# Two halves of an image mixer on one Trainium2 core: second images of one half beside the first images of the other, first modes of both at once, earlier parameters, larger loads

## Chip, cores, metric

The kernel runs on 1 core of one Trainium2 chip. The metric is device time in microseconds (us), lower is better. All runs compared here are of the fast state. In the text PE is TensorE (matmul), DVE is VectorE, ACT is ScalarE, SP is SyncE, whose queue issues most loads; a "half" is 128 of the 256 channels, or, of a tile, 1024 of its 2048 columns; "modes" are the low frequencies of the images. Of the tiles, gs holds the modes of one block, yA the forward products of one block, Yd is the copy of these in device memory, YT that copy loaded again, and f1ps the products made from YT; g10 and g11 are the syntheses of the first modes of half 0 and half 1, g20 and g21 those of the second modes.

## The reference, cut to what matters

```python
# layer 0 (attention over rows) makes x1; neither it nor the first part of layer 1 changes
attn = instance_norm(attn + tokens, attn_norm_w, attn_norm_b)      # the kernel's y, scaled by lam
attn = attn.reshape(b * (C // 4), 4, H, W)                          # four channels are mixed
h0 = instance_norm(attn, norm2_w, norm2_b)
h1 = fno_layer(h0, mix_wr[0], mix_wi[0], ..., (H, W), norm=True, act=True)   # first modes, first images
h2 = fno_layer(h1, mix_wr[1], mix_wi[1], ..., (H, W), norm=True)             # second modes, second images
out = instance_norm(h2, mon_w, mon_b) + attn
return x1 + out
# fno_layer: forward FFT, 32x16 modes times weights, inverse FFT, norm, plus a 1x1 skip; act is gelu
```

Each group of four channels is on its own, so the kernel works on two halves of the channels in turn.

## The kernel before

```python
def first_modes(a):                     # spectrum of half a, synthesis to Gd1 in device memory
    ...                                 # scalars, scaling of Fy, products (mix_modes)
    synth_modes(wp, psum, Zj, P, h.Gd1, f"g1{a}")          # 16 stores on the SP queue

def first_images(a):
    def begin(b):
        ...                             # y block: resident for a == 0 and b >= 4, else a 1 MB load
        load_modes(gs, h.Gd1, b)
        ps = [psk.tile([P, 512], FP, tag="k", ...) for j in range(4)]
        skip(ps, by_turn(yt), h.bl0, False)
        image(ps, gs, bs4, slice(0, P))
        for j in range(4):
            nc.scalar.activation(by_turn(hb[b])[:, j], ps[j]..., AF.Gelu)
    for b in range(17):
        if b < 16:
            begin(b)
        if b > 0:
            ...                         # transposes, statistics, forward products of block b-1
            nc.scalar.copy(yA, psA)
            nc.scalar.dma_start(h.Yd[:, b - 1, :], yA)

def second_modes(a):
    for c in range(4):
        for hc in range(2):
            t = yp.tile([P, 2, 4, P], FP, tag="YT", ...)
            for j in range(4):
                for r in range(2):      # 64 loads of 64 KB a half, 32 partitions each
                    f0 = 32 * j + 16 * r + 4 * c
                    nc.sync.dma_start(t[32 * j : 32 * j + 32, r],
                        h.Yd[f0 : f0 + 4, 8 * hc : 8 * hc + 8, :].rearrange("f b (n t) -> (b n) f t", n=4))
        ...                             # f1ps: products with efwd, copied to F
    Z, left = mix_modes(wp, psum, F, 1, f"z{a}")
    synth_modes(gp, psum, [Z], P, h.Gd2, f"g2{a}")
    ...

def second_images(a):                   # pools: op bufs=2, opp bufs=8 (PSUM)
    for b in range(16):
        gs = wp.tile([P, 4, P], FP, tag="gs", ...);  load_modes(gs, h.Gd2, b)
        yt = wp.tile([P, NB], FP, tag="yt", ...);    nc.sync.dma_start(yt, ydv[:, a, px])
        xt = wp.tile([P, NB], FP, tag="xt", ...);    nc.sync.dma_start(xt, x1v[:, a, px])
        ps = [psk.tile([P, 512], FP, tag="k", ...) for j in range(4)]
        skip(ps, by_turn(hb[b]), blk[1], False)
        image(ps, gs, bs4, slice(0, P))
        for j in range(4):
            nc.scalar.activation(by_turn(hb[b])[:, j], ps[j]..., AF.Identity, bias=c0, scale=kap)
        nc.vector.scalar_tensor_tensor(xt, yt, lam, xt, ALU.mult, ALU.add)
        nc.vector.tensor_tensor(xt, xt, hb[b], ALU.add)
        nc.scalar.dma_start(outv[:, a, px], xt)

for a in range(2):
    first_modes(a); first_images(a); second_modes(a); second_images(a)
```

## Time and profile before

| | before |
|---|---|
| median, range of 3 runs | 3392.2 us, 3390.0 to 3397.3 |
| profiled run | span 3403.0 us |
| layer 0 and attention of layer 1, not touched | up to 2182 us |
| y of both halves, from its first to its last product | 264 us |
| first modes, first images, second modes, second images of half 0 | 72, 140, 89, 167 us |
| the same of half 1 | 58, 138, 85, 166 us |

A row of the windows view, as the prediction shows it, gives one stretch of the span. One reads it from the right: a high DMA share (0.89 in second images) suggests that transfers are the bound (the runs below show that it need not be so), a PE time close to the length (124.14 of 140.00 us in first images) suggests that PE is, and a row in which neither is high (40.77 of 71.70 us and 0.24 in first modes) suggests a chain of dependent steps. A row of the waits view names who waited, what ended the wait, and total, count and longest.

### The profile page before, as it was taken

Reading aid. Unit: us, or ns where it says so; the run is one execution under the profiler, and the core shown is the slowest. Engines: PE = TensorE matmul, PEld = TensorE weight load, DVE = VectorE, ACT = ScalarE, POOL = GpSimd, SP = SyncE. Lnnn points to the kernel's source line nnn. Section 1 sums busy time; section 2 is a strip of 40 time slices with the busy share of each in tenths; the row PEclk is TensorE's granted clock in tenths of the full one; section 3 lists DMA queues with packets and bytes.
Section 4 is the critical chain, followed back from the end, with each engine's and each line's share of the span. In section 5 each row is a group of like instructions: output and inputs, shape, how many; then the busy total and the mean of one; then the engine's idle time right before and its main releaser. Section 6 shows DMA issues by size and latency. Waiting matters only on the chain. (4 is left out here: it accounts for less than half of the span.)

```text
span 3403.0 us, 71671 instructions
## 1 busy us (share of the span) xinstructions
PE 2964.7 (87%) x30109; PEld 2003.0 (59%) x30109; DVE 1908.9 (56%) x2848; ACT 1240.2 (36%) x2277; POOL 1002.0 (29%) x807
## 2 busy tenths in 40 slices
PE   6799999999999999999996785989967776569675
PEld 5577777777777777777774474744443344344444
DVE  7566666666666666666665125746654434435344
ACT  0355555555555555555552001100013212133022
POOL 0255555555555555555552002000000000000000
PEclk9899999999999999999997955999978877589765
DMA  9222212111111111111110000278723248654298
GB/s 372 93 62 62 62 62 62 62 62 60 63 59 62 62 60 62 62 62 62 62 53 13 0 20 0 87 282 294 291 69 125 76 152 324 236 185 161 87 330 329
DMA packets 224524, 398.55 MB, mean 117 GB/s; under 512 B 23589, under 2 KB 181752, under 8 KB 197064
## 3 DMA queue, kind: packets, MB, share of 16 engines
q1 hardware_dynamic: 210376, 318.43, 28.0%
q10 hardware_dynamic: 13824, 75.50, 5.6%
q8 instruction: 239, 3.92, 0.5%
q14 instruction: 85, 0.70, 0.1%
HBM read 259.63 MB, written 134.22 MB: 116 GB/s over the span
## 5 line engine op out<-in xcount | busy, mean ns | idle before, releaser
L263 POOL TENSOR_TENSOR e<-e,b1T 128x1024 f32<-128x1024 f32 x256 | 609.4, 2381 | 104.5 <-ACT e L261 104.4
L282 DVE RECIPROCAL rd<-av 128x256 f32<-128x256 f32 x256 | 448.2, 1751 | 0.0
L284 POOL TENSOR_TENSOR og<-t,rd 128x256 f32<-128x256 f32 x256 | 185.8, 726 | 612.1 <-PE sc L253 593.9
L312 ACT COPY U<-u 128x129 f32<-128x129 f32 x256 | 99.4, 388 | 719.4 <-DVE stats L311 719.4
L281 DVE SCALAR_TENSOR_TENSOR t<-gate,av 128x256 f32<-128x256 f32 x256 | 107.9, 422 | 401.0 <-ACT gate L244 383.3
L262 DVE TENSOR_TENSOR e<-sc,b1T 128x1024 f32<-128x1024 f32 x256 | 309.0, 1207 | 2.5 <-PE sc L253 2.5
L253 PE MATMUL sc<-qkT 32*128 32x256 f32 x4096 | 293.3, 400 | 0.1
L264 ACT ACTIVATE e<-e 128x1024 f32<-128x1024 f32 x256 | 276.0, 1078 | 0.5 <-DVE e L262 0.4
L275 PE MATMUL av<-e,v 128*32 128x256 f32 x4096 | 274.7, 385 | 0.5 <-POOL e L263 0.5
L261 ACT ACTIVATE e<-sc 128x1024 f32<-128x1024 f32 x256 | 271.5, 1060 | 3.8 <-PE sc L253 3.7
L275 PE MATMUL av<-e,eb 128*32 128x256 f32 x4096 | 268.2, 379 | 0.0
L979 PE MATMUL yps<-xt,mpT 128*128 128x512 f32 x512 | 230.8, 604 | 11.6 <-issue 11.6
L287 POOL TENSOR_TENSOR xb<-xt,bo 128x256 f32<-128x256 f32 x256 | 187.0, 731 | 121.0 <-DMA kt<-in_L_conv_kv_x_dram 121.0
L240 DVE TENSOR_TENSOR v<-gv,eb 128x256 f32<-128x256 f32 x256 | 108.8, 425 | 198.6 <-PE gv L237 198.5
L944 PE MATMUL h2ps<-k_bsyn,gs 32*128 32x128 f32 x1024 | 128.7, 402 | 98.8 <-DMA gs<-Gd 98.7
L253 PEld LDWEIGHTS sc<-qkT 32*128 32x128 f32 x4096 | 184.9, 184 | 37.8 <-issue 0.6
L944 PEld LDWEIGHTS h2ps<-k_bsyn,gs 32*128 32x128 f32 x1024 | 119.9, 290 | 142.7 <-DMA gs<-Gd 116.5
L293 PEld LDWEIGHTS wo<-wo_half,og 128*128 128x128 f32 x1024 | 133.8, 190 | 107.0 <-issue 104.2
L275 PEld LDWEIGHTS av<-e,eb 128*32 128x32 f32 x4096 | 133.0, 110 | 88.2
L293 PE MATMUL wo<-wo_half,og 128*128 128x128 f32 x1024 | 182.7, 301 | 1.9 <-POOL og L284 1.9
L275 PEld LDWEIGHTS av<-e,v 128*32 128x32 f32 x4096 | 106.8, 109 | 129.8 <-ACT xnT L219 80.5
L1316 ACT ACTIVATE blocks<-h2ps,col 128x512 f32<-128x512 f32 x128 | 94.8, 776 | 236.0 <-PE h2ps L944 205.8
(494 smaller groups left out, 5393.8 us busy)
## 6 DMA issues: line engine op xcount, KB each, us to landing
y<-yd SPq DMA_DIRECT2D x52, 1024.0 KB
xb<-in_x_dram SPq DMA_DIRECT2D x32, 1024.0 KB
xt<-in_x_dram SPq DMA_DIRECT2D x128, 256.0 KB
kt<-in_L_conv_kv_x_dram SPq DMA_DIRECT2D x128, 256.0 KB
x1d<-x SPq DMA_DIRECT2D x256, 128.0 KB
xt<-x1d SPq DMA_DIRECT2D x32, 1024.0 KB
x<-x1d SPq DMA_DIRECT2D x32, 1024.0 KB
out_dram<-x ACTq DMA_DIRECT2D x32, 1024.0 KB
```

The source lines that it names most:

```text
L253: nc.tensor.matmul(sc[h // 2][:, h % 2, c * 256 : (c + 1) * 256], qkT[p, 256 + c * P : 256 + (c + 1) * P], qkT[p, 0:256], start=True, stop ...
L261: nc.scalar.activation(e[1], s1[1], AF.Exp)
L262: nc.vector.tensor_tensor(e[0], s1[0], b1[0], ALU.add)
L263: nc.gpsimd.tensor_tensor(e[1], e[1], b1[1], ALU.mult)
L264: nc.scalar.activation(e[0], e[0], AF.Exp)
L275: nc.tensor.matmul(ps[hd, den * 256 : (den + 1) * 256], w, r["e"][h // 2][:, h % 2, c, :], start=(c == 0), stop=(c == 1),)
L282: nc.vector.reciprocal(rd, ps[:, 256:512])
L284: nc.gpsimd.tensor_tensor(r["og"], t, rd, ALU.mult)
L287: nc.gpsimd.tensor_tensor(r["xb"], r["x"], bc(bo, 1, 2), ALU.add)
L293: nc.tensor.matmul(ps[:, j * P : (j + 1) * P], r["og"][:, j * P : (j + 1) * P], wo, start=True, stop=True)
L944: nc.tensor.matmul(ps[j][:, n * W : (n + 1) * W], gs[q, n, tt], bs[q, :], start=False, stop=(n == 3))
L979: nc.tensor.matmul(ps[j].rearrange("p (n w) -> p n w", w=W), mpT[:, sc, tt], by_turn(xt[:, sc])[:, j], start=(sc == 0), stop=False,)
```

## The change

The intent: first modes of both halves in one stage; the first half's output beside the second half's first images, since one is bound by transfers and the other by PE; parameters and the spectrum fetched in front of y; 16 loads of YT in place of 64; y and x1 in halves of a block, so that all of it fits.

```diff
+Fyd = dram.tile([P, 4, 2, NT], FP, name="Fyd")      # Fy stored here, loaded as F0 in front of y
...
-            def first_modes(a):
+            def first_modes():                        # both halves: one scaling, one mix_modes of width 256
...
+                        for a, h in enumerate(halves):
+                            synth_modes(wp, pss, Z[:, :, :, a * P : (a + 1) * P], P, h.Gd1, f"g1{a}", turned=True)
...
                     for b in range(17):
                         if b < 16:
+                            if beside is not None:
+                                beside(b, op, psk)
                             begin(b)
...
+                        YT = yp.tile([P, 2, 2, 16, P], FP, name=f"YT_{a}")
+                        for hc in range(2):
+                            for j in range(4):
+                                for r in range(2):
+                                    (nc.sync if r else nc.scalar).dma_start(
+                                        YT[32 * j : 32 * j + 32, hc, r],
+                                        h.Yd[32 * j + 16 * r : 32 * j + 16 * r + 16, 8 * hc : 8 * hc + 8, :].rearrange(
+                                            "f b (n t) -> (b n) f t", n=4))
...
-            def second_images(a):
+            def second_images(a, b, wp, psk):
+                for s in range(2):
+                    px = slice(b * NB + s * half, b * NB + (s + 1) * half)
+                    yt.append(wp.tile([P, half], FP, tag="yo", name=f"y4_{a}_{b}_{s}", bufs=2))
+                    nc.sync.dma_start(yt[s], ydv[:, a, px])
+                    xt.append(wp.tile([P, half], FP, tag="xo", name=f"x4_{a}_{b}_{s}", bufs=3))
+                    nc.sync.dma_start(xt[s], x1v[:, a, px])
+                gs = wp.tile([P, 4, P], FP, tag="gs3", name=f"gs3_{a}_{b}", bufs=2)
+                load_modes(gs, h.Gd2, b)
...
+            first_modes()
+            first_images(0)
+            second_modes(0)
+            first_images(1, beside=lambda b, wp, psk: second_images(0, b, wp, psk))
+            second_modes(1)
+            with tc.tile_pool(name="op", bufs=2) as wp, tc.tile_pool(name="opp", bufs=8, space=PSUM) as psk:
+                for b in range(16):
+                    second_images(1, b, wp, psk)
```

## The prediction

> **What bounds the kernel now.** I read the page's slices first. The change touches nothing before 2180 us, so I cut the rest, with the chain of work that ended last, into stages and asked for the busy time of each engine in each. The stages are: first half's y (the input of both halves' work), then for each half first modes, first images, second modes, second images. Columns: stretch; length; busy us of PE, weight loads, DVE, ACT, POOL; granted clock; DMA share; GB/s.
>
> ```profile
> 2215.00:2488.00 273.00, 263.96 (x1536) 126.98 (x1536) 156.05 (x252) 0.00 (x0) 0.00 (x0) 0.98 0.76 274
> 2488.00:2559.70 71.70, 40.77 (x588) 26.96 (x588) 34.56 (x101) 9.95 (x20) 0.00 (x0) 0.68 0.24 74
> 2559.70:2699.70 140.00, 124.14 (x1920) 58.01 (x1920) 72.44 (x113) 51.47 (x97) 0.00 (x0) 0.96 0.28 90
> 2699.70:2789.00 89.30, 54.21 (x676) 37.05 (x678) 25.91 (x56) 7.29 (x13) 0.00 (x0) 0.72 0.36 103
> 2789.00:2955.90 166.90, 102.07 (x948) 64.47 (x945) 74.30 (x32) 47.30 (x64) 0.00 (x0) 0.64 0.89 325
> 2955.90:3013.60 57.70, 37.43 (x582) 23.95 (x582) 23.59 (x45) 8.08 (x15) 0.00 (x0) 0.74 0.27 76
> 3013.60:3151.80 138.20, 122.69 (x1920) 57.34 (x1920) 72.47 (x113) 51.47 (x97) 0.00 (x0) 0.97 0.54 181
> 3151.80:3237.00 85.20, 52.47 (x658) 35.80 (x658) 25.97 (x56) 7.29 (x13) 0.00 (x0) 0.76 0.34 100
> 3237.00:3403.00 166.00, 110.46 (x960) 71.23 (x960) 74.31 (x32) 47.50 (x64) 0.00 (x0) 0.59 0.89 331
> ```
>
> The reader should see three kinds of stage. First images (140.0 and 138.2 us) are held by PE, with the DMA half idle. Second images (166.9 and 166.0) are held by the DMA at a share of 0.89. The modes (71.7, 89.3, 57.7, 85.2) are held by neither: they are chains of short dependent steps. In the chain of work, second images repeat one loop, and the queue's waits name its hinge:
>
> ```profile
> 2800.30 8.26 DMA out_dram<-x
> 2808.64 8.20 DMA x<-x1d
> 2816.92 2.36 DVE x L1320
> 2819.37 2.30 DVE x L1321
> 2821.70 7.40 DMA out_dram<-x
> ...
> SPq L1311 <- DMA out_dram<-x: 75.0, 8, 10.3
> ```
>
> A store must land before its buffer can be loaded again. Two buffers, a loop of some 21 us, so 10.4 us for each of 16 blocks. The timeline of second modes shows a third cost, the 64 small loads, and that of first modes the accumulation through PE:
>
> ```profile
> 2701.78 31.05 SPq L1250 DMA_DIRECT2D YT<-Yd  x64
> 2734.09 2.79 PE L1262 MATMUL f1ps<-YT,k_efwd 128*32 128x128 f32 x48 [2.76 <-DMA YT<-Yd]
> 2507.32 17.07 PE L1057 MATMUL x0acc<-x0m,ident 128*128 128x512 f32 x32 [2.87 <-DVE x0m L1056]
> ```
>
> [...]the 64 KB loads ran at 132 GB/s and share 0.46, and 325 GB/s at 0.89 makes 365 at full share. [...]the first x0acc instructions are 0.85 us apart, later ones 0.43; the window of the small loads had a granted clock of 0.50.
>
> **The change part by part.**
>
> Parameters and F0 ahead of y. The spectrum of y now goes to DRAM and back (1 MB each way), and some ten small loads stand before y's first load. They fall next to the g0 stores, where the DMA ran at 299 GB/s and 0.87, so perhaps +5 us before y. At its other end they save: before, the scalars waited for parameters and ended at 2502.3, and the chain without them would end near 2499: -3.
>
> First modes at once. For both halves after y's last statistics at 2490.6: scalars to 2499; broadcast, copy and product of double width, 6.5 us (1.2 became 2.4 for the product); 32 accumulations of 0.857 us warm, plus 3 cold, 30.5 (one half took 17.1); squares, energies, reciprocal root and scaling of double width, 12.5 (before about 8.7); that is 2548.5. Then g1 of half 0 and of half 1 at 18.7 us each, as before: 2586. The reversed views replace copies of some 2.4 us a half, and I take the matmuls to cost the same. Before, the first image matmul stood at 2564.3, after 7.5 us of waiting for stores and loads; these now lie under half 1's g1. So +22 us here and the whole second stage of 57.7 gone: **-36**.
>
> Larger loads. 64 issues of 0.485 us become 8 on each of two queues, with the same 4.2 MB in 512-byte runs. By 132/0.46 these cannot pass 287 GB/s: 14.6 us and a latency near 2. But now the four groups of f1ps, 3.9 us each at half clock, all wait for the last load: about 10 us, half of it warm. F was ready 35 us after the last store; now about 27. The accumulation then starts warm (-2) and the 16 one-column matmuls leave the energy chain (-1.8). **About -11 for each half, -22 in all**. The later sum with its reciprocal is hidden under the g2 stores.
>
> Second images of half 0 beside first images of half 1. The bytes of one block, in MB: y 1.05, x1 1.05, out 1.05, y for the first images 1.05, two mode blocks 0.52, spectrum 0.26: 4.98, 79.7 in 16 blocks. At 365 GB/s that is 218 us, at the 328 of before 243 (15.2 a block). PE has 7.93 (its period in the first images' timeline) plus 1.18 and 1.17 for skip and image, 10.3 a block. DVE has 4.5 and 4.65, ACT about 6. So the DMA is the bound and the stages cannot merge to the longer of the two. There is one more tie: the first image of block b overwrites what the output of block b has just read, and both share 4 PSUM buffers; skip and image 2.4, eviction 2.8, sums 2.3, gelu 2.1 in a row, about 10, fits below 15 but makes the loads' slack small. I choose 16.0 us a block and 9 for ends: 265 against 305.1: **-40**.
>
> Second images of half 1. The same bytes in halves of 0.5 MB; three x halves in place of two whole buffers. The loop may take 3 x 5.2 = 15.6 us; half transfers of some 4 to 6 us and 2.35 of DVE fit. I take +2.
>
> Sum: +5 -3 (already in the 22) leaves +5 -36 -22 -40 +2 = -91, so 3392 - 91 = **3301**, rounded to 3300.
>
> **The rivals.** (1) *A wait takes the place of the one removed.* In program order gs now follows the second x half, which waits for a store of the block before. If the queue keeps that order, each block is store 3 to 4, gs issue and landing 5 to 6, image and eviction 4, sum 1.2: 14 to 16 us in place of 10.4, costing the last stage 60 to 80 us and the middle one 20. Then 3375 to 3400. Against it: the order in the trace is not that of the source. At the start of the first layer two xt loads went ahead of a kt load whose buffer was taken:
>
> ```profile
> 120.38 0.47 SPq L208 DMA_DIRECT2D kt<-in_L_conv_kv_x_dram  x1
> 120.89 0.98 SPq L206 DMA_DIRECT2D xt<-in_x_dram  x2
> 124.07 0.37 SPq L208 DMA_DIRECT2D kt<-in_L_conv_kv_x_dram  x1
> ```
>
> So a ready load is moved ahead. For it: in second images the order was gs, y, x throughout, although gs was free earlier. I give this rival one chance in four. (2) *DMA stays full.* With work of PE, DVE and ACT under it, the middle stage could run at 365 GB/s: 220 to 235, the total near 3265. Against it: fewer bytes can be in flight, five halves of 0.5 MB of y and x where before it was four whole MB, so a late block is caught up less easily. One in six. (3) *The loads are hidden or bound anyway*: if f1ps stays cold or 512-byte runs crawl on two queues, second modes gain nothing, 3320.
>
> **Range and chances.** The 2% border is 3324. The main path lies at 3280 to 3325, rival 2 below it, rival 1 on or above 3370. That gives 3250 to 3375 for 8 in 10; faster 0.70, same 0.26, slower 0.04 (only if rival 1 also hits the middle stage hard).
>
> **What would show it.** Right: one stretch of first modes near 95 us; YT landing in about 17 us; 16 blocks of 15 to 16.5 us with a DMA share near 0.9; a last stage of 160 to 172. Wrong: gs loads issued after the second x half and evictions waiting for gs, with a share well under 0.8; DVE or ACT standing behind a late x half while turns wait; g1 over 20 us a half with reversed views; y starting more than 10 us late.

## The result

| | before | after |
|---|---|---|
| median | 3392.2 us | 3373.4 us |
| range, runs | 3390.0 to 3397.3, 4 | 3366.7 to 3375.7, 4 |
| profiled span | 3403.0 us | 3364.9 us |

The ratio is 0.9939, with a 95% interval from 0.9920 to 0.9958: a gain of 19 us, clear of the noise and far short of the 91 predicted. A ratio is the mean time of one kernel's fast runs over that of the other's in the same rounds, so it is not quite the ratio of the two medians. The profiled run of before (3404.8 us) lies above the range of the timed ones, that of after (3366.7 us) at the lower end of its own, and the unchanged part up to 2180 us was 12 us shorter in the run after; so I compare stage by stage, not by the spans.

This is the windows view of the kernel after, cut at the same events as the prediction's table of before; the columns are the same. The stages are y, first modes of both halves, first images of half 0, second modes of half 0, the combined stage, second modes of half 1, second images of half 1.

```profile
2206.90:2479.30 272.40, 263.31 (x1536) 127.06 (x1536) 156.12 (x252) 0.00 (x0) 0.00 (x0) 0.98 0.77 278
2479.30:2583.80 104.50, 64.50 (x1114) 40.39 (x1114) 51.32 (x98) 12.93 (x24) 0.00 (x0) 0.78 0.30 92
2583.80:2722.50 138.70, 122.71 (x1920) 57.38 (x1920) 72.62 (x113) 51.45 (x97) 0.00 (x0) 0.97 0.27 91
2722.50:2804.80 82.30, 45.32 (x626) 32.98 (x626) 25.99 (x57) 7.28 (x13) 0.00 (x0) 0.77 0.53 117
2804.80:3084.80 280.00, 213.02 (x2912) 91.57 (x2912) 150.73 (x177) 95.97 (x161) 0.00 (x0) 0.88 0.81 282
3084.80:3162.70 77.90, 44.04 (x594) 33.48 (x594) 24.02 (x44) 7.08 (x12) 0.00 (x0) 0.78 0.52 110
3162.70:3364.90 202.20, 122.46 (x1024) 75.54 (x1024) 79.67 (x77) 47.56 (x65) 0.00 (x0) 0.58 0.78 271
```

First modes took 104.5 us for both in place of 71.7 and 57.7. The combined stage took 280.0 in place of 166.9 and 138.2. Second modes fell by 7 us each. But the last row, where the code does the same work as before, grew from 166.0 to 202.2 us, while its DMA share fell from 0.89 to 0.78: transfers had become less busy, so something waited.

The chain of work that ended last, in the last stage of the kernel after (start, length, what), answers to the loop that the prediction shows:

```profile
3237.14 5.11 DMA out_dram<-x
...
3242.33 3.65 DMA x<-x1d
...
3247.26 1.23 DVE x L1320
3248.51 6.46 DMA out_dram<-x
```

A store of a half, then a load into its buffer, then the sums, then the next store: the same loop, with pieces of half the size. It is gone through once a block, every 11.4 to 12.8 us, where the kernel before needed 10.4 us a block. The waits of the load queue and of PE's weight loads between 3200 and 3350 us:

```profile
SPq L1306 <- DMA out_dram<-x: 71.5, 25, 7.5
PEld h2ps L949 <- DMA gs<-Gd: 70.4, 13, 7.1
```

L1306 loads x1; gs are the modes. Loads wait for stores, and the images wait for their modes. The queue's issues in the same place (start, length, what) show why both go together:

```profile
3247.37 0.32 SPq L1304 DMA_DIRECT2D y<-yd  x1
3247.74 1.81 SPq L965 DMA_DIRECT2D gs<-Gd  x4
3255.02 0.35 SPq L1306 DMA_DIRECT2D x<-x1d  x1
```

The modes were moved ahead of the last x half, but they stand behind the second y half, and that waits for DVE's sum of the block before.

### The profile page after: what moved, and what is told of

Its sections match the earlier page's. It is cut to its first block, busy times and chain, and to the rows that moved or that the text cites. A ratio compares the mean times of both kernels' runs of the same rounds, so it can differ in the third digit from the quotient of the medians.

```text
span 3364.9 us, 71699 instructions
## 1 busy us (share of the span) xinstructions
PE 2926.9 (87%) x30059; PEld 1956.8 (58%) x30059; DVE 1910.7 (57%) x2873; ACT 1231.2 (37%) x2266; POOL 1002.3 (30%) x807
## 5 line engine op out<-in xcount | busy, mean ns | idle before, releaser
L1025 PE MATMUL yps<-xt,mpT 128*128 128x512 f32 x512 | 230.2, 603 | 13.2 <-DMA xt<-x1d 13.2
L1319 DVE SCALAR_TENSOR_TENSOR x<-y,col,x 128x1024 f32<-128x1024 f32 x64 | 82.2, 1284 | 175.9 <-DMA x<-x1d 163.8
L1025 PEld LDWEIGHTS yps<-xt,mpT 128*128 128x128 f32 x512 | 95.6, 192 | 125.1 <-issue 113.3
L233 PEld LDWEIGHTS gv<-wT_wv,kvT 128*128 128x128 f32 x1024 | 154.7, 191 | 13.1
```

Source lines behind the costliest of these rows:

```text
L233: nc.tensor.matmul(ps[:, 256 + c * P : 256 + (c + 1) * P], kvT[:, c * P : (c + 1) * P], wT["wv"], start=True, stop=True,)
L1025: nc.tensor.matmul(ps[j].rearrange("p (n w) -> p n w", w=W), mpT[:, sc, tt], by_turn(xt[:, sc])[:, j], start=(sc == 0), stop=False,)
```

## The experiments

Four questions: where the last stage lost 36 us, what the combined stage is bound by, what the larger loads are bound by, and what stood between first modes and first images. Stage times below are read from the profiled run, from event to event: the last stage from its first load to the end of the span, the combined stage from its first load to the first load of YT after it. By that rule the kernel after has 201.0 and 285.8 us, and the two stages that the combined one replaces take 311.6 us in the run e4_apart. The combined stage is the least steady part: seven runs with its code and loads unchanged show 285.8 to 298.0 us, so a difference under some 10 us there is not read as an effect.

| run | median us | ratio to before (95%) | stage in question |
|---|---|---|---|
| e1_last_whole | 3347.0 | 0.9858 (0.9843 to 0.9873) | last 168.8 |
| e2_last_modes_first | 3353.5 | 0.9878 (0.9863 to 0.9893) | last 174.4 |
| e3_last_more_buffers | 3352.1 | 0.9878 (0.9863 to 0.9893) | last 172.5 |
| e4_apart | 3368.6 | 0.9924 (0.9910 to 0.9937) | two stages apart 311.6 |
| e5_small_loads | 3359.4 | 0.9898 (0.9883 to 0.9913) | YT to store 62.7, 64.8 |
| e6_long_runs | 3346.7 | 0.9863 (0.9844 to 0.9882) | YT to store 58.8, 59.1 |
| e10_wide_loads | 3384.7 | 0.9975 (0.9966 to 0.9983) | YT to store 81.0, 81.3 |
| e11_two_quarters | 3335.4 | 0.9843 (0.9824 to 0.9862) | YT to store 58.2, 58.3 |
| e13_merged_rows | 3354.0 | 0.9888 (0.9873 to 0.9903) | YT to store 48.3, 48.2 |
| e7_no_x | 3396.6 | 1.0000 (0.9990 to 1.0009) | combined 342.2 |
| e9_part_x | 3333.1 | 0.9826 (0.9807 to 0.9845) | combined 274.6 |
| e12_images_order | 3388.8 | 0.9991 (0.9979 to 1.0002) | combined 332.5 |
| e14_four_x | 3339.4 | 0.9841 (0.9824 to 0.9857) | combined 286.0 |
| e15_modes_first | 3340.7 | 0.9848 (0.9835 to 0.9862) | combined 286.2 |
| e16_free | 3333.6 | 0.9827 (0.9807 to 0.9847) | combined 278.5 |
| e8_late_half | 3339.2 | 0.9835 (0.9820 to 0.9851) | y to first images 97.7 |
| e17_all | 3318.0 | 0.9768 (0.9754 to 0.9783) | all |
| e18_own_image | 3311.0 | 0.9752 (0.9738 to 0.9765) | combined 292.8 |

e7, e9 and e16 give a wrong result on purpose; all others are correct. "YT to store" runs from the first load of YT to the first store of the synthesis that follows, for half 0 and half 1; after the change it is 60.0 and 60.2 us, before it 66.2 and 67.9.

### The last stage: order of the loads, or number of buffers

```diff
 e1: the loop over the last 16 blocks calls the form before (one load of y, one of x1, bufs=2, modes first)
-                    second_images(1, b, wp, psk)
+                    second_whole(1, b, wp, psk)
 e2: for a == 1 alone, load_modes stands ahead of the loads of y and x1
 e3: for a == 1 alone
-  tag="yo", bufs=2      tag="xo", bufs=3
+  tag="yo", bufs=4      tag="xo", bufs=4
```

> The changed kernel, with the last stage alone (second images of the second half) in the form of the kernel before: one 1 MB load of y and one of x1 a block, two buffers of each, the modes loaded first. Both theories (order of the loads; number of buffers) expect the last stage to come back from 202 us to about 166 us, so the total to fall by 30 to 36 us against the changed kernel: about 3340 us, 0.985 of before. If the last stage stays at 200 us, its loss is not of the form of its loads at all (then the lower granted clock, 0.56, would be next).

> The changed kernel with one edit in the last stage: the modes (gs) of a block are loaded in front of its halves of y and x1 instead of behind them; halves and buffers stay (2 of y, 3 of x1). Theory of the order (the modes wait in the load queue behind a half that waits for a store): the last stage falls from 202 to 166-175 us, total about 3340-3346. Theory of the buffers (store lands, x1 loads, VectorE, store, three halves in turn): the last stage stays at 195-203 us, total about 3370.

> The changed kernel with one edit in the last stage: four buffers for halves of y and four for halves of x1 (the bytes of the form before), modes still loaded behind them. Theory of the buffers: the last stage falls from 202 to about 166-172 us, total about 3340. Theory of the order: it stays at 190 us or more, total 3360-3373.

e1 brought the stage back to 168.8 us, against 164.7 before the change. This is its row of the windows view:

```profile
3175.20:3344.00 168.80, 114.39 (x1024) 72.68 (x992) 75.72 (x41) 47.52 (x64) 0.00 (x0) 0.59 0.88 324
```

The DMA share is back at 0.88, at the same low clock of 0.59 (0.59 before, 0.58 in the kernel after), so the clock is not the cause. The surprise is in the other two. Neither theory wins: the order alone gave back 26.6 of 36 us with the buffers left scarce, and the buffers alone gave back 28.5 us with the modes left behind. (By the medians against the kernel after, e1, e2 and e3 give back 26, 20 and 21 us; the expectation of e15 writes 22 of 27.) By these runs the loss needs both, a load that waits and something urgent behind it. Either edit shortens what the images wait for their modes: between 3200 and 3320 us PE's weight loads waited 58.2 us for them in the kernel after, 50.2 in e2 and 51.4 in e3. With more buffers (e3) the longest wait of an x1 load for a store was 5.1 us, in place of 7.5.

### Beside each other, or apart

```diff
 e4: e1, and the second images of half 0 on their own in the form before
+            with tc.tile_pool(name="op0", bufs=2) as wp, tc.tile_pool(name="opp0", bufs=8, space=PSUM) as psk:
+                for b in range(16):
+                    second_whole(0, b, wp, psk)
-            first_images(1, beside=lambda b, wp, psk: second_images(0, b, wp, psk))
+            first_images(1)
```

> The first run's kernel (last stage in the form before) and in addition the second images of the first half on their own in the form before, in front of the first images of the second half: so nothing beside anything. If the combined stage of the changed kernel (286 us) is worth what its trace says, the two stages take 166 + 138 = 304 us here and the total is 18 us over the first run of this job, about 3358. If the combined stage was worth the 40 us of the prediction, 40 us over it; if nothing, the same.

It took 21.5 us more than e1, measured on the same chip in the same rounds. In the traces the two stages took 311.6 us against 291.4. So the combination is worth about 20 us, half of the 40 predicted.

### What bounds the combined stage

```diff
 e7:  x1 not loaded; DVE takes y twice and writes into the x tile
-     nc.vector.scalar_tensor_tensor(xt[s], yt[s], lam, xt[s], ALU.mult, ALU.add)
+     nc.vector.scalar_tensor_tensor(xt[s], yt[s], lam, yt[s], ALU.mult, ALU.add)
 e9:  an eighth of x1 loaded (bufs=2) and read eight times; y (bufs=3) is worked on in place and stored
 e12: DVE's sums and the store of block b come after the turn and statistics of block b-1
 e14: tag="xo", bufs=4 in the combined stage
 e15: load_modes of the second images ahead of y and x1 in the combined stage
 e16: e15 and e9 together, with bufs=5 for the y that carries the result
```

> A wrong result on purpose: the kernel of e1_last_whole, whose combined stage does not load x1 (VectorE takes y in its place; instructions are otherwise the same). 16 MiB of 76 MiB fall away in that stage. Theory of the bandwidth (the stage is bound by the bytes at about 300 GB/s): the combined stage falls by 16.8 MB / 300 GB/s = 56 us, from 291 to about 236 us, total about 3291. Theory of the order (it is bound by loads that wait for stores in one queue and by engines that wait in order, at whatever rate): it falls by less than 30 us, total above 3317.

This run is a lesson in experiments. With 16 MiB less to move the stage took 51 us *more* than in e1. The edit had shifted the wait. Before it, a load in the queue waited for the store that frees the x tile; after it, DVE itself did, in order, 46.4 us in 8 waits between 2850 and 3050 us, and the transposes' copies and the statistics stood behind it. The run says nothing on bytes, so I made a cleaner one.

> A wrong result on purpose, cleaner than the last one: the kernel of e1_last_whole, whose combined stage loads an eighth of each half of x1 (read eight times over by VectorE). y takes the three buffers and is worked on in place, so the queue of loads still waits for the stores and VectorE does not. 14.7 MB of 80 MB fall away. Theory of the bandwidth: the combined stage falls by 14.7 MB / 300 GB/s = 49 us, from 291 to about 242 us, total about 3298. Theory of the order (waits of queue and engines, not bytes): it falls by less than 20 us, or not at all, total above 3327.

With 14.7 MB fewer the stage fell by 16.8 us against e1 (by 11 against the shortest unchanged one), not by 49. The waits stayed in place but not quite in size: between 2850 and 3050 us the load queue waited 80.0 us for stores, in e1 62.1, and DVE 34.0 us for loads, in e1 42.3. The DMA share fell, while the blocks came at nearly the same pace. This is the steady part in the kernel after, and then in e9:

```profile
2850.00:3050.00 200.00, 155.72 (x2242) 65.80 (x2237) 111.62 (x131) 71.02 (x121) 0.00 (x0) 0.91 0.89 305
```

```profile
2850.00:3050.00 200.00, 156.49 (x2277) 67.38 (x2270) 116.76 (x136) 73.78 (x124) 0.00 (x0) 0.92 0.77 260
```

In the totals the gain is smaller still: in the same rounds e11, whose combined stage is unchanged, has a ratio of 0.9843 beside 0.9826 here. So the bytes alone are not what holds the stage, although the DMA share of 0.89 in the kernel after looks like a bound.

> The kernel of e1_last_whole, with another order in the combined stage: VectorE's part of a block's output (lam*y + x1, plus the image) comes after the transposes and statistics of the block before, not ahead of them, so that these no longer stand behind a wait for x1. Theory of the order: the 16.0 us a block of the steady part fall to 14-15 us, the combined stage from 291 to 260-275 us, total 3317-3331. Theory of the bandwidth: the steady part stays at 16.0 us a block, total 3340-3350.

I had expected a gain and got a loss of 41 us. The waits between 2850 and 3050 us show how (DVE's sums, and the load queue):

```profile
DVE x L1324 <- DMA x<-x1d: 92.9, 15, 9.6
SPq L1310 <- DMA out_dram<-x: 109.6, 20, 8.8
```

In e1 the same two rows read 42.3 and 62.1 us. A later sum means a later store, a later free buffer, a later load, and then a later sum again. The place of the sums in DVE's order is part of the loop.

> The kernel of e1_last_whole with one number changed in the combined stage: four buffers for halves of x1, not three. Theory of the ring (a half of x1 is loaded only when the store of the third half before it has landed; three halves in 24 us): four halves in 24 us are 12 us a block, so that the next bound, some 14 us, holds: the combined stage falls from 291 to 260-272 us, total 3316-3328. Rival (bytes, or VectorE and TensorE in order, hold the 16 us): it stays over 284 us, total 3340-3350.

> The kernel of e1_last_whole with the modes of the second images loaded ahead of the halves of y and x1 in the combined stage too. In the last stage this edit gave 22 of 27 us. If the modes behind a waiting half hold the combined stage as well, it falls from 291 to 272-280 us, total 3328-3336; if only the ring of x1 holds it, it stays at 287-294 us, total 3342-3350.

Both stages are at the lower edge of the spread of unchanged ones (286.0 and 286.2 us), and the intervals of the totals overlap that of e1. Neither is an effect that I would claim; neither is the 20 us that would make it the bound. The edit that repaired the last stage does not repair this one.

> A wrong result on purpose: the kernel of e15_modes_first, with x1 cut to an eighth in the combined stage as in e9_part_x and five buffers for the halves of y that carry the result. Ring, order of the modes and bytes are eased at once. Theory that three bounds of like size lie on each other and the loads are all of them: the stage falls from 286 to 230-245 us (TensorE is busy some 12.8 us a block), total 3280-3297. Theory that the engines' own chain (images, scaling, gelu, turn, products through 8 PSUM banks, in order) holds about 15-16 us a block: the stage stays at 262-278 us, total 3314-3332.

All three were to be eased at once: 278.5 us, 13 us less than e1, and no more than e9 alone gave (the totals are 3333.6 and 3333.1). From the first to the fifteenth copy of yA (2848.31 and 3075.40 us) the blocks are 16.2 us apart; the same count gives 16.3 in e9 and 16.9 in e1. I took this to leave only the engines' own steps, one behind the other: second image, scaling on ACT, first image into the same PSUM buffers, gelu on ACT, copies, transposes, products. The trace does not bear that out. More buffers did not take the waits away; between 2850 and 3050 us DVE and the load queue still waited:

```profile
DVE y L1320 <- DMA y<-yd: 43.9, 14, 5.3
SPq L1308 <- DMA out_dram<-y: 48.4, 17, 7.2
```

DVE's row is as long as that of e1 (42.3 us in 14 waits). And the blocks have two paces: by the copies of yA some are 13.6 us apart, others 17 to 21, and in one of the slow ones (2976.59 to 2997.18 us) DVE waits 5.22 us for y. So the engines' steps can turn out a block in 13.6 us, and waits for loads are not excluded as what stretches the others.

> The kernel of e17_all, where in the combined stage ScalarE writes the scaled second image into a buffer of its own, so that gelu of the first image needs no longer wait for VectorE's sum (and so for x1). To make room, x1 has three buffers again, the modes of the second images and yA one each. Theory of the link: the blocks that take 18 to 20 us fall to the 13.6 us of the fast ones, the combined stage from 286 to 250-268 us, total 3282-3300. Rival (another link of the chain, or the bytes, hold it as well; or the smaller buffers take back what is gained): the stage stays over 276 us, total 3308-3322.

```diff
 e18: e17 (below), with a tile of its own for the scaled second image
+                im = wp.tile([P, NB], FP, tag="im", name=f"im_{a}_{b}", bufs=1)
-                        by_turn(hb[b])[:, j], ps[j]..., AF.Identity, bias=c0, scale=kap,
+                        by_turn(im)[:, j], ps[j]..., AF.Identity, bias=c0, scale=kap,
-                    nc.vector.tensor_tensor(xt[s], xt[s], hb[b][:, s * half : (s + 1) * half], ALU.add)
+                    nc.vector.tensor_tensor(xt[s], xt[s], im[:, s * half : (s + 1) * half], ALU.add)
```

The theory of that link found no support: the stage took 292.8 us against 285.9 in e17, within its spread, though gelu no longer had to wait for what the sums read. (The smaller buffers may have taken back what the tile gave; no run parts the two.) (The total of 3311 is 7 us under e17, but not through this stage; the ratios' intervals overlap.) The timeline of e18 shows what I had overlooked:

```profile
2957.55 2.35 DVE L1325 TENSOR_TENSOR x<-x,im 128x1024 f32<-128x1024 f32 x2
2958.80 1.47 ACTq L1326 DMA_DIRECT2D out_dram<-x  x2
2960.32 2.06 ACT L1171 ACTIVATE blocks<-ups 128x512 f32<-128x512 f32 x4 [3.55 <-DVE x L1325]
```

The stores of the output are issued by ACT, in its own order. It stands at the issue until DVE's sum is done, and gelu comes 0.05 us after the second issue. So gelu still waits for the sums and through them for x1, by way of the queue that ACT serves. This is read from one trace and was not tested; a run that issues those stores from another queue would tell. What holds the combined stage at 16 us a block therefore stays open; it is not the bytes alone, not the number of x buffers alone and not the order of the modes alone, and a tile of its own for the second image did not free it.

### The loads of YT

```diff
 e5:  64 loads of 64 KB on SP, as before
 e6:  Yd laid out as [block, quarter, row, t]: loads read runs of 8 KB, stores write runs of 512 bytes
 e10: e6, and 4 loads YT[:, hc, r] whose source has the dimensions j (4), (b n) (32), (f t) (2048)
 e11: the two queues take different j at a time
-     for j in range(4): for r in range(2): (nc.sync if r else nc.scalar)...
+     for r in range(2): for j in range(4): (nc.sync if j % 2 else nc.scalar)...
 e13: Yd as [2, 4, 32, 32, P], so that j and (b n) merge into one dimension of 128; 4 loads, and 4 stores a block
```

> The kernel of the run e1_last_whole (last stage in the form before), with the 64 small loads of YT on one queue as before the change in place of 16 larger ones on two. The prediction put the larger loads at 11 us a half: then the total rises by 22 us over e1_last_whole, to about 3369. The traces of before and after show the time from the first YT load to the first Gd2 store 66-68 us against 60: then it rises by 10 to 14 us, to about 3359. If the gain of the stage came from its other edits, by less than 5.

The larger loads are worth 12.4 us in the medians (13.6 by the ratios, as the two runs were on different chips), 8 in the two stretches of the trace (each counted up to the next stage's first load): real, and half of what I predicted. In the kernel after, the first issue of YT and the main part of f1ps read:

```profile
2724.65 13.62 SPq L1238 DMA_DIRECT2D YT<-Yd  x8
2749.29 8.24 PE L1250 MATMUL f1ps<-YT,k_efwd 128*32 128x128 f32 x224 [8.32 <-DMA YT<-Yd]
```

24.6 us pass from the first issue to the last landing, where I had put 17. f1ps then runs for 8 us behind it, while before it ran between the small loads.

> The kernel of e1_last_whole with Yd laid out anew in device memory (block, quarter, row, mode), so that the 16 loads of YT read runs of 8 KB where they read 512-byte runs, and the stores of Yd write runs of 512 bytes. Theory of the runs: the landing of YT is set by 4,096 runs of 512 bytes in each half; it falls from 25 us to 7-10 us, the stretch from first load to first Gd2 store from 60 to about 45 us in each half; the 16 stores with short runs cost the combined stage up to 9 us; total 3320-3330. Theory of the issues (16 issues of 1.7 us on two queues, or a fixed latency): the stretch stays over 55 us and the total at 3340-3350.

Runs sixteen times as long changed little: the stretch fell by one us. The windows view of the landing in the kernel after, and then in e6 (length, busy times, clock, DMA share, GB/s):

```profile
2727.00:2749.00 22.00, 1.93 (x32) 1.50 (x32) 0.00 (x0) 0.00 (x0) 0.00 (x0) 0.50 1.15 179
```

```profile
2732.00:2752.00 20.00, 1.94 (x32) 1.51 (x32) 0.00 (x0) 0.00 (x0) 0.00 (x0) 0.50 0.93 195
```

The engines are about as busy as in e13 below (share 1.00), at less than half its 423 GB/s (the share adds up the time of all packets, so over 1 some overlapped). The length of the runs is not the cause: 179 GB/s with runs of 512 bytes, 195 with runs of 8 KB. (A half has 8,192 runs of 512 bytes, not the 4,096 of the expectation; and where that of e13 writes a share of 0.99, these windows read 0.93 to 1.19.)

> The kernel of e1_last_whole (512-byte runs, 16 loads of 32 partitions), with the loads shared out so that the two queues write different quarters of the partitions at a time; before, both wrote the same quarter. Theory of the quarter: the landing falls from 25 to about 15-18 us, the stretch from first load to first Gd2 store from 60 to 50-54 us a half, total 3328-3336. Rival (runs or issues bind as well): the stretch stays at 58-60 us, total 3342-3350.

> The kernel of e6_long_runs (8 KB runs), with 4 loads of YT of 1 MB over all 128 partitions in place of 16 loads that each write 32 partitions. The run e6 showed that long runs alone leave the landing at 24 us. Theory: what holds the landing is that the loads under way write one quarter of the partitions; with all 128 it falls to 7-10 us, the stretch from first load to first Gd2 store from 59 to about 44 us in each half, total about 3315-3322. Rival: the landing of 2 MB is bound elsewhere (reading what was just written, or a rate of 180-200 GB/s for this read), the stretch stays at 57-60 us, total 3342-3350.

e11 moved the stretch by 2 us, so the theory of the quarter seemed dead, and e10 made things worse. The landing in e10:

```profile
2732.00:2768.00 36.00, 1.94 (x32) 1.51 (x32) 0.00 (x0) 0.00 (x0) 0.00 (x0) 0.50 0.25 102
```

The DMA share is 0.25, where e6 has 0.93: the 16 engines together were busy for a quarter of the time. The source's outermost dimension is 4 in these loads; which engines were busy, and why no more, is not shown. So e10 tested something else than I meant. Nor did e11 settle the quarter: with two quarters at a time (0 and 1, then 2 and 3) it ran at 197 GB/s, beside 179 and 195 with one at a time; loading quarters 0 and 2 together was not tried, and why two were little faster than one is not shown. e13 gives all 128 partitions and an outermost dimension of 128.

> The kernel of e1_last_whole, with Yd laid out so that YT comes in 4 loads of 1 MB, each over 128 partitions in one merged dimension with 8 KB runs (the loads of e10 had an outer dimension of 4 and moved 98 GB/s at a DMA share of 0.22; the stores of Yd are 4 a block here). Theory: writing 32 partitions at a time held the landing at 25 us (about 190 GB/s for 4.2 MB at a share of 0.99); with 128 it falls to 11-14 us, the stretch from first load to first Gd2 store from 60 to 46-50 us a half, total 3320-3328, if the smaller stores cost the images nothing. Rival: the read itself holds it, the landing stays over 20 us, total 3340 or more.

Its landing:

```profile
2749.00:2757.00 8.00, 1.94 (x32) 1.51 (x32) 0.00 (x0) 0.00 (x0) 0.00 (x0) 0.50 1.00 423
```

YT lands at 423 GB/s, more than twice the rate, and the stretch falls by 12 us in each half, as the theory said. e13 also makes 4 loads of 1 MB out of 16 of 256 KB, so the size of a load is a rival to the partitions. A kept trace speaks against it: at the start of the kernel after, eight loads of the same 256 KB, but over 128 partitions and in runs of 1 KB, moved 307 GB/s:

```profile
120.00:126.00 6.00, 4.57 (x18) 3.42 (x18) 0.00 (x0) 2.11 (x5) 1.41 (x2) 0.58 0.94 307
```

The total of e13 rose nevertheless by 7 us: four stores a block in place of one, issued by ACT (1.8 to 3.5 us a block in first images and up to 7.1 us in the combined stage, in place of 0.33), made first images 16 us longer (152.2 against 136.3) and the combined stage 13 us.

### Between first modes and first images

```diff
 e8: g11, the synthesis of half 1's first modes, moved into second_modes(0), ahead of mix_modes, with its copies on ACT alone
-                        for a, h in enumerate(halves):
-                            synth_modes(wp, pss, Z[:, :, :, a * P : (a + 1) * P], P, h.Gd1, f"g1{a}", turned=True)
+                        synth_modes(wp, pss, Z[:, :, :, 0:P], P, halves[0].Gd1, "g10", turned=True)
```

> The kernel of e1_last_whole, with the synthesis of the second half's first modes (g11: 16 stores) taken out of the joint stage and done inside the second modes of the first half, beside the products there. Theory: g11 stands between the first half and its images, because the first loads of images come behind its 16 stores: the stretch from the end of y to the first images falls from 116 to 96-100 us, the second modes of the first half grow by at most 5 us, total 3328-3335. Rival: the products and Z of both halves are what costs, g11 is hidden: the stretch falls by under 6 us, total 3341-3350.

The stretch from the end of y to the first images fell from 116.1 to 97.7 us, as expected. But second modes of half 0 grew by 12.6 us, not by 5: there g11 stood on PE ahead of the products, which began at 2758.75 us behind its last matmuls. The 18 us were moved more than saved; the total fell by 8 us. Nor did the wait for the first loads go: PE stood 12.3 us behind the last matmuls of g10 here, as it did 12.2 us behind those of g11 in e1. In the kernel after, the SP queue shows where g11 hurts:

```profile
2547.69 15.65 SPq L521 DMA_DIRECT2D Gd<-g10gt  x16
2565.11 15.03 SPq L521 DMA_DIRECT2D Gd<-g11gt  x16
2583.11 0.34 SPq L1161 DMA_DIRECT2D y<-yd  x1
```

The first load for the images of half 0 is issued after all 16 stores of half 1, since its buffer lies where g11's tiles were (that queue waited 2.7 us for the last of these stores).

### The mends together

```diff
 e17: e1 + e14 + e15, and
+  ahead = _Held(tc.tile_pool(name="hpa", bufs=2))    # buffers of first_images(0), opened before first_modes()
+  low = ...tile_pool(name="low4", bufs=1, side="right")
+  h.Yd = dram.tile([16, 4, P, P], ...)               # as e6: one store a block
+  YT[:, hc, r] <- h.Yd[8 * hc : 8 * hc + 8].rearrange("b n (j r f) t -> r (b n j) (f t)", j=4, r=2)[r]
+  tf.transpose(3, 4, 5, 2, 0, 1)                     # rows of the constant efwd in the order (b n j)
```

> All mends in one kernel: last stage in the form before; in the combined stage modes first and four buffers for x1; YT in 4 loads of 1 MB over 128 partitions in one merged dimension, with one store of Yd a block (the rows of the constant efwd are put in the same order); buffers of the first half's images opened ahead of the first modes, so that its first loads go ahead of g11's stores. From the runs: 3347 of e1_last_whole, less 7 to 12 in the combined stage, less 24 for YT, plus up to 5 for the stores with short runs, less 8 to 12 for the first images: about 3310, between 3298 and 3322. If the mends only shift waits, over 3325.

3318.0 us, ratio 0.9768, correct: it beats both kernels, by 77 and by 55 us. By the trace YT to store takes 49.9 and 49.2 us (from 59.9 and 60.5 in e1), first images stay at 138.2, y to first images is 109.2 (from 116.1). Here are the issue of YT and the main part of f1ps, to set beside the rows of the kernel after:

```profile
2727.42 0.82 SPq L1242 DMA_DIRECT2D YT<-Yd  x2
2740.77 8.87 PE L1254 MATMUL f1ps<-YT,k_efwd 128*32 128x128 f32 x224 [2.70 <-DMA YT<-Yd]
```

13.4 us from issue to landing, in place of 24.6. e18 was built on this and is the fastest kernel measured, 3311.0 us, ratio 0.9752.

## Why the prediction was wrong, step by step

Measured sizes are stage differences between the traces of before and after.

| step | predicted | measured |
|---|---|---|
| parameters and F0 ahead of y | +5 | +4 |
| first modes at once: on half 0 | +22 | +33 |
| first modes at once: stage of half 1 gone | -58 | -58 |
| larger loads, both halves | -22 | -14 |
| second images beside first images | -40 | -25 (-20 from e1 to e4) |
| last stage in halves | +2 | +36 |
| sum | -91 | -24 |

The spans of the two traces differ by 38 us, of which 12 lie before the change; y and the first images of half 0 make up the 2 that are missing from the sum. The medians differ by 19 us. The combined stage, the least steady part, is where a single trace is most likely to be off.

- **Parameters**: right. 39.0 us from the last spectrum products to y's first product became 42.8.
- **First modes at once**: the mechanism was right, and up to the end of g11 so was the working: accumulations 29.2 us for 30.5 predicted, the matmuls of both syntheses 33.9 for 37.4. The step that failed is "these now lie under half 1's g1". The first loads came after g11's stores, and PE stood 11.9 us behind g11's last matmuls until the modes had landed. e17 confirms it: with early buffers that wait is gone and the stretch fell by 7 us, since g11 itself ended some 5 us later there. e8 is no test of this step, only of g11's own length: the stretch fell by 18 us, but a wait of 12.3 us stayed.
- **Larger loads**: the term that was mis-sized is the landing, "14.6 us and a latency near 2"; it measured 24.6. I had divided a rate by a busy share, 132/0.46. But with the engines full (1.15) these loads, each over only 32 partitions, ran at 179 GB/s. e6 (195 GB/s) excludes the runs, and the loads of 256 KB over 128 partitions (307 GB/s) exclude the size; e13 and e17 remove the loss with loads over all 128 partitions, at 423 and 419 GB/s. Why loads over fewer are slow is not shown.
- **Beside each other**: the step that failed is "the DMA is the bound". The pace of 16.0 us a block was met, by accident: the copies of yA in the kernel after lie 15.9 us apart on average. e9 shows that the bytes alone do not set it: with 18% fewer the stage gave back 17 us of the 49 that a bound of bytes would give. What sets it stays open. Nor was 365 GB/s, an estimate from a rate and a share (325 at 0.89), the limit of the transfers: the trace of before has loads at 420 GB/s and a share of 1.01 between 60 and 80 us. The other mis-sized term is the "9 for ends": 285.8 us less 16 times 15.9 leaves 31. From the stage's first load to the first yA 43.9 us pass, and in the last 37 us the DMA moves only 108 GB/s: second images run ahead at the start, and at the end only first images are left. That lag of some 22 us more than planned is what the combined stage missed by. e4 confirms that about 20 of the 40 us remain.
- **The last stage**: the step that failed is "the loop may take 3 x 5.2 = 15.6 us; half transfers and DVE fit". It leaves out that the two stores of a block are issued together (ACT issues both within 1.47 us), so that three buffers hold one block and a half and the loop is gone through once a block. I had given rival 1, modes queued behind a waiting half, one chance in four. It came, with 12.4 us a block and not 14 to 16 (the pieces given there add up to 13.2 to 15.2), perhaps because the modes were in fact moved ahead of the last half. e1, e2 and e3 show that it took order and scarce buffers together.

## What to carry to other kernels

Before a tile is cut into halves to save room, write out the ring: which loads wait for which stores, and what stands behind them in the same queue; keep small urgent loads ahead of those that can wait (in the last stage here the order alone gave back 26.6 of 36 us). A busy share near 1 is not a rate near the limit (179 GB/s at 1.15, 423 at 1.00), and a stage with a high share need not be bound by its bytes (at 0.89, 18% fewer bytes gave 17 us of 49): cut the bytes alone, with every wait left where it is, before calling it so. After a run that should ease a wait, look in its trace whether the wait went. And when two stages are laid side by side, count the lag at both ends besides the pace in the middle.

## What the loads of YT show in a profile

- Loads over 32 partitions, on one or two quarters at a time, ran at 179 to 197 GB/s (the kernel after, e6, e11), loads over 128 at 423 (e13) and 419 (e17). The DMA share reads 0.93 to 1.19 in the first case and 1.00 and 0.99 in the second, so that a rate divided by the share misled me.
- 8 loads took 13.6 us to issue on the SP queue, beside a landing of 24.6 us; with runs of 8 KB in place of 512 bytes (e6) 13.1 us; the same bytes in 2 loads over 128 partitions (e17) 0.8 us. So it is not the number of runs; whether the issue waits for the transfers themselves was not tested.
